# One PSUM bank in four quarters for the small users of the gated stages, and the planner's new price for float32r matmuls

## The chip, the cores and the metric

The kernel runs on 1 core of one Trainium2 chip. The metric is device microseconds of the program; the profile is one execution, taken by the hardware profiler, with times counted from the start of its span. PE is TensorE (PEld its weight loads), DVE is VectorE, ACT is ScalarE, POOL is GpSimd, SP is SyncE, which issues most DMAs. PSUM, where PE writes its results, has eight banks of 512 float32 words in each of 128 partitions; DVE and ACT read and write it too.

## The reference

The input is 4 sequences of 1024 rows of 128 values. Six stages change it in place, each by a residual add. Cut to what matters:

```python
x = x + 0.5 * ffn0(layernorm(x))     # 128 -> 512 -> 128, gelu
x = x + attn0(layernorm(x))          # 16 heads of 8
x = x + 0.5 * ffn0(layernorm(x))
x = x + 0.5 * ffn1(layernorm(x))     # gated stage, below
x = x + attn1(layernorm(x))          # 16 heads of 64, causal
x = x + 0.5 * ffn1(layernorm(x))     # gated stage

def ffn1(x):                         # two layers, l = 0 and 1
    for l in range(2):
        h = shift_token(x)           # upper 64 values from the row before
        q, k, v = split(h @ wqkv[l])             # 8 heads of 64
        q, k = rotary(l2norm(q) * qs[l], l2norm(k) * ks[l])
        x = x + local_attention(q, k, v) @ wo[l]  # windows of 64, own and previous
        h = layernorm(shift_token(x)) * lg[l] + lb[l]
        a, g = split(h @ w1[l] + b1[l])           # 341 each
        x = x + (a * gelu(g)) @ w2[l] + b2[l]
    return x
```

## The kernel before, in words

**Tiles.** `X[i]` holds 512 rows as four parts of 128, for i from 0 to 7. A gated stage (`ffn1`, run as `ffn1a` and `ffn1b`) works on `Y(i)`, one part at a time in the attention: `attend(t0, l, g, ...)` is one frame, 32 parts in each of two layers, 64 frames in a stage. The gated feed-forward, `gated(t0, l, i)`, takes a whole block of four parts; it is done in groups of blocks, between runs of frames, and there are 16 of them in a stage.

**One frame.** `turn_x` transposes the frame's shifted part into PSUM; `upper` (ACT) and `lower` (DVE) copy it out as two float32r parts of one number. `project` makes three times three matmuls of 128x512. `square` (ACT), `turn_a` and `turn_b` (DVE) read a projection; `add` and `normalise` (POOL) finish q and k. `sums` (DVE) writes the 16 squared norms of a frame into PSUM, where `variance` (DVE) has put one or two variances of layer norms; `clip` (DVE), `log`, `guess` (ACT) and `newton` (three DVE instructions) make reciprocal roots of all of them in place. `turn` and `untwist` transpose q and k, `score` makes the scores in two banks of their own, `top`, `exp`, `inverse`, `norm_e` the softmax, `turn_e` and `untwist_e` transpose it, `weigh` multiplies by v. `project_out` makes the 128x128 output product, `collect` (DVE) adds it. A frame also turns, by `turn_x`, one part for the gated feed-forward. There, `bias2` (POOL) adds a bias to `Y(i)` and has to wait until the block's `shift` (five or more DMAs on SP) has read it; `hidden`, `gelu`, `gate`, `down` and `collect` follow. `shift_of` is a small product that `glu_weights` makes four times in a stage.

**Who decides the order.** Every function is recorded with `at(t, f)` as a step. Then `Plan.order` lists them anew: a step becomes ready when the steps that it needs are done and its buffers have a place; engines take the earliest ready step, ties by due time. `best_order` does this six times, each with due times from the try before, and keeps the order with the earliest end by the planner's own clock. `cost` prices an instruction for that clock. So any price and any place moves steps in all stages. The order is then the program's: each engine runs its instructions in it (`follow`), and stands at a wait.

**Where PSUM results go.** All of PSUM is one tile, `wordsP`. `bank(tag, slots)` gives a buffer a place among the banks named, here banks 0 to 5 for everything in a gated stage but the scores (6 and 7). A place is a list of `Cell`s, one to each bank. A buffer keeps its place until its last reader is done. `order` also keeps, for each cell, when each engine last used it, so that a step on another engine starts after that:

```python
for b in banks:
    for c in b.slot:
        for x, end in c.last.items():
            if x != e:
                t = max(t, end + self.X_LAT)
```

All recorded instructions are issued at one line of `issue` (L241), so the groups below are told apart by engine, tile and shape.

Of the kernel before, what the change touches and what calls it, by code (L numbers as in the profile page):

```python
# [11 lines left out]
F32 = mybir.dt.float32  # L12
# [9 lines left out]
D = 128  # L22
EPS = 1e-5
NEG = -1e30
MARGINS = (0.0,)

BANKS, ROUNDED, SWING, WORDS = 4096, 14208, 10240, 28744
# [17 lines left out]
def flat(x):  # L45
    return x.rearrange("p a b -> p (a b)")


def free_size(x):
    return math.prod(x.shape[1:])  # L50
# [42 lines left out]
class Plan:  # L93
# [13 lines left out]
    def __init__(self, ctx, tc):  # L107
        nc = tc.nc
        self.tc, self.ctx, self.pools, self.swing = tc, ctx, {}, ExitStack()
        self.steps, self.recording, self.cur, self.states = [], True, None, []  # L110
        self.scratch, self.owner = bacc.Bacc("TRN2", target_bir_lowering=False, num_devices=1), {}
        self.tags = {}
        self.bank_cells = [Cell("P", 512 * k, 512 * k + 512) for k in range(8)]
        self.masks, self.last, self.table = {}, {}, None
        self.pe, self.ac, self.ve = Engine(self, nc.tensor, "P"), Engine(self, nc.scalar, "A"), Engine(self, nc.vector, "D")
        self.gp, self.sy = Engine(self, nc.gpsimd, "G"), Engine(self, nc.sync, "S")
# [38 lines left out]
    def place(self):  # L155
# [8 lines left out]
        for g in sorted(tags, key=lambda g: (g.last - g.first < 0.9 * total, -g.words, g.first)):  # L164
# [3 lines left out]
            for _ in range(min(g.bufs, len(g.buffers))):  # L168

                for margin, kind in ((m, kind) for m in MARGINS for kind in kinds):  # L170
                    lo = 0
# [20 lines left out]
    def bank(self, tag, slots, shape=(128, 512), dt=F32, turns=True):  # L192
        if self.recording:
            g = self.tags.setdefault(tag, Tag(tag))
            n = (math.prod(shape[1:]) * (2 if dt == BF else 4) + 2047) // 2048
            g.turns = turns
            if not g.slots:
                g.words, g.bufs, g.kind = 0, 0, "P"
                g.slots = [self.bank_cells[k : k + n] for k in slots]
            return self.record("P", g, shape, dt)  # L200
        return self.shaped(shape, dt)

    def await_place(self, x):

# [111 lines left out]
    def cost(self, key, name, args, kw, out, ins, mode):  # L316

        n = free_size(out)
        if key == "P":
            if name == "transpose":  # L320
                return 0.109 if args[1].dtype == F32 else 0.056
            x = args[2]
            if x.dtype == F32:
                t = 4 * free_size(x) / 2400 + 0.009
            elif x.dtype == FR:
                t = max(free_size(x) / 2400 + 0.015, 0.112)
            else:
                t = free_size(x) / 2400 + 0.003

            return t * mode[0] * mode[1] / 128**2  # L330
        if key == "A":
            extra = sum(isinstance(kw.get(z), bass.AP) for z in ("bias", "scale", "accum_out"))
            return 0.055 + n / 1200 + 0.093 * extra
        if key == "D":
            if name in ("tensor_reduce", "bn_stats"):
                n = free_size(ins[0])
            psum = any(self.owner[x.tensor.name].space == "P" for x in (out, *ins) if x.tensor.name in self.owner)
            if name == "tensor_copy" and (not psum or out.dtype == ins[0].dtype == BF):
                n /= 2
            return 0.068 + n / 960 + 0.06 * sum(isinstance(x, bass.AP) and free_size(x) == 1 < n for x in args[1:])  # L340
        if key == "G":
            if name == "tensor_tensor":
                return 0.15 + n * (1.67 if any(x.ap[-1][0] == 0 for x in ins) else 2.1) / 1000
            return 0.245 + n * 0.83 / 1000
        return math.prod(out.shape) * 4 / 360e3
# [302 lines left out]
class Macaron:  # L648
# [491 lines left out]
    def attn1(self, ph, T0, lead):  # L1140
# [197 lines left out]
        def heads(t0, n, i):  # L1338
# [16 lines left out]
            def top(z, k):  # L1355
# [3 lines left out]
                if parts[z].stop < TK:  # L1359
# [4 lines left out]
                    out=sc(), in0=sc(), in1=W["cm"][:, 512 - w : 512], scale=-1.0,  # L1364
                    scalar=V["m", K, k][0][:, 0:1] if two else -NEG,
                    op0=ALU.add, op1=ALU.min, accum_out=o,
# [141 lines left out]
    def ffn1(self, ph, T0, last):  # L1508

        pre = ph + "."  # L1510
        V, at, pe, ac, ve, gp, sy, tile_ = self.begin(pre)
        a, plan = self.a, self.plan
        NB, G, HC = self.NBLK, self.NBLK * 4, 114
        bank = lambda: plan.bank(pre + "p", [0, 1, 2, 3, 4, 5], (128, 4, 128))
        dm = sy.dma_start
        W = {}

# [58 lines left out]
        def glu_weights(t0, l):  # L1576
            def new():
                W["lg", l], W["lb", l] = tile_([128, 1], "lg"), tile_([128, 1], "lb")
                dm(out=W["lg", l], in_=a["L1_ffn_ln_g"][l].unsqueeze(1))
                dm(out=W["lb", l], in_=a["L1_ffn_ln_b"][l].unsqueeze(1))  # L1580

                W["w1h", l], W["w1l", l] = tile_([128, 2, 3 * HC], "w1h", 1, FR), tile_([128, 2, 3 * HC], "w1l", 1, FR)
                W["b2", l] = tile_([128, 128], "b2")
                dm(out=W["b2", l], in_=a["L1_ffn_b2"][l].unsqueeze(0).broadcast_to([128, 128]))

            def clear():
                W["b1", l], W["w2", l] = tile_([128, 6], "b1"), tile_([128, 3, 128], "w2")
                gp.memset(W["b1", l], 0.0)
                gp.memset(W["w2", l][96:128, 2, :], 0.0)

            def second():
                for c in range(3):
                    m = min(HC, 341 - HC * c)
                    dm(out=W["w2", l][0:m, c, :], in_=a["L1_ffn_w2"][l][HC * c : HC * c + m, :])

            def clear_first(z):
                W["w1", l, z] = tile_([128, 512], "raw", 3)
                gp.memset(W["w1", l, z][:, 341:342], 0.0)

            def fetch(z):  # L1600
                dm(out=W["w1", l, z][:, 0:341], in_=a["L1_ffn_w1"][l][:, 341 * z : 341 * z + 341])
                for c in range(3):
                    m = min(HC, 341 - HC * c)
                    o = 341 * z + HC * c
                    dm(out=W["b1", l][0:m, 3 * z + c : 3 * z + c + 1], in_=a["L1_ffn_b1"][l][o : o + m].unsqueeze(1))

            def high(z):
                ac.activation(W["w1h", l][:, z, :], W["w1", l, z][:, 0 : 3 * HC], AF.Copy, scale=W["lg", l])

            def low(z):  # L1610
                w, h = W["w1", l, z][:, 0 : 3 * HC], W["w1h", l][:, z, :].bitcast(F32)
                ve.scalar_tensor_tensor(W["w1l", l][:, z, :], w, W["lg", l], h, ALU.mult, ALU.subtract)

            def shift_of(z):
                pb = W["pb", l, z] = flat(bank())
                for c in range(3):
                    pe.matmul(pb[0:HC, c : c + 1], W["w1", l, z][:, HC * c : HC * c + HC], W["lb", l], start=True, stop=True)

            def bias(z):
                b1, zs = W["b1", l], slice(3 * z, 3 * z + 3)  # L1620
                ve.tensor_tensor(b1[0:HC, zs], W["pb", l, z][0:HC, 0:3], b1[0:HC, zs], ALU.add)

            for j, f in enumerate((new, clear, second)):
                at(t0 + j, f)
            for z in range(2):
                for j, f in enumerate((clear_first, fetch, high, low, shift_of, bias)):
                    at(t0 + 3 + 4 * z + j, f, z)
# [56 lines left out]
                at(t + 0.01, shift_first, key, i)  # L1684

        def turn_x(key, src):
            V["t", key] = bank()
            pe.transpose(V["t", key][:, 0, :], src(), self.ident)

        def upper(key, dst):  # L1690
# [43 lines left out]
        def attend(t0, l, g, xn, xx, xg):  # L1734

            at = lambda t, *z: plan.at(warp(t), *z)
            i, t = divmod(g, 4)
            n = g % 8
            K = (l, g)
# [16 lines left out]
            width = 16 + len(extra)  # L1756

            def sums_of():
                if ("ss", K) not in V:

                    V["ss", K] = [flat(b)[:, 32 * j : 32 * j + width] for b in (bank(),) for j in range(2)]
                return V["ss", K][0]

            def sums():
# [146 lines left out]
                ac.copy(V["oT", K], V["o", K])  # L1911

            def project_out():
                pw = V["w", K] = bank()
                for c in range(4):
                    pe.matmul(pw[:, 0, :], V["oT", K][:, c, :], W["wo", l][:, c, :], start=(c == 0), stop=(c == 3))

# [38 lines left out]
            for k, x in enumerate(extra):  # L1956
                z = x[0]
# [93 lines left out]
        for f in range(2 * G):  # L2051
            l, g = tile_of(f)
# [5 lines left out]
            if g % 4 == 3:  # L2058
# [3 lines left out]
                q = next(q for q in groups if l * NB + i in q)  # L2062
                k = groups.index(q)
# [37 lines left out]
def _constants():  # L2101
# [5 lines left out]
    c = {"c_ident": np.eye(128, dtype=f), "c_blk8": (i[:, None] // 8 == i[None, :] // 8).astype(f)}  # L2107
    c["c_causal"] = np.where(i[None, :] > i[:, None], f(NEG), f(0))
    p, kk = (i % 64)[:, None], i[None, :]
# [55 lines left out]
```

## Time and profile before

| what | value |
| --- | --- |
| median of 3 runs | 3156.43 us (3156.14 to 3158.03) |
| the profiled execution | 3154.36 us, span 3152.6 us |
| granted TensorE clock, mean | 0.987 |
| PE, ACT, DVE, POOL busy | 94%, 78%, 70%, 46% of the span |
| `ffn0a`, `attn0`, `ffn0b` | to about 605 us |
| `ffn1a` | about 605 to 1345 us |
| `attn1` | about 1345 to 2400 us |
| `ffn1b` | about 2400 us to the end |

The stages overlap at their borders. A line of the page's groups reads: line, engine, operation, tiles out<-in, shapes, count, then busy time, mean ns of one, and the idle time of the engine just before them with what ended it. A line of a timeline reads: start, length, engine, operation, count, and in brackets the idle time before it with its releaser.

### The profile page before, as it was taken

The page shows a single profiled execution, that of the slowest core. Times are in us where ns is not written, and L with a number is a line of the kernel's source. Part 1 is how long each engine was busy: PE and PEld are TensorE (multiplying, and loading weights), DVE is VectorE, ACT ScalarE, POOL GpSimd, SP SyncE. Part 2 cuts the span into 40 slices and gives each one's busy share as a digit, 9 for nine tenths or more (in the row PEclk, how much of TensorE's full clock was granted, in tenths as well). Part 3 has the DMA queues.
Part 4 walks back from the last instruction along what each step waited for, and adds up shares of the span by engine and source line. Part 5 has one row for each costly group of instructions (what it writes and reads, how often), then busy time and mean ns, then how long its engine had stood idle before and what let it go on. Part 6 is the DMA issues. An engine that isn't in the chain of part 4 may idle for free.

```text
span 3152.6 us, 75646 instructions
## 1 busy us (share of the span) xinstructions
PE 2973.4 (94%) x26596; PEld 2112.5 (67%) x26596; DVE 2201.5 (70%) x6896; ACT 2461.8 (78%) x6856; POOL 1455.6 (46%) x1622
## 2 busy tenths in 40 slices
PE   8999999988899999899999999999999898999988
PEld 6322222677777777777777777777777677777767
DVE  8343341567767676888888877878787777776775
ACT  6999999678878687767777777777777788787873
POOL 1000000178958586533333333333344898685871
PEclk9999999999999999999999999999999999999999
DMA  1000000122212121122222221222231322122211
GB/s 41 1 1 1 1 3 11 33 67 58 55 40 60 42 59 35 48 59 51 56 46 46 53 46 44 54 46 50 48 81 38 75 57 56 38 59 49 57 42 34
DMA packets 209425, 137.26 MB, mean 44 GB/s; under 512 B 148548, under 2 KB 164632, under 8 KB 209048
## 3 DMA queue, kind: packets, MB, share of 16 engines
q1 hardware_dynamic: 208328, 131.87, 18.4%
q8 instruction: 213, 3.49, 0.4%
q0 software_dynamic: 720, 0.56, 0.1%
q14 instruction: 164, 1.34, 0.1%
HBM read 17.58 MB, written 2.10 MB: 6 GB/s over the span
## 4 chain that ended last, share of the span: by engine, by line
PE 66%; DVE 15%; ACT 8%; POOL 5%; issue 4%; SPq 1%; DMA 1%; DVEq 0%; ACTq 0%; POOLq 0%
PE wordsP L241 66%; DVE wordsS L241 9%; ACT wordsS L241 6%; POOL wordsS L241 4%; DVE words L241 3%; DVE wordsP L241 2%; ACT words L241 2%; POOL words L241 1%; SPq L241 1%; DVE wordsR L241 1%; DMA wordsS<-wordsS 0%; DMA words<-L_ffn_w 0%; ACT wordsR L241 0%; DMA wordsS<-L_attn_x 0%; DVEq L241 0%
## 5 line engine op out<-in xcount | busy, mean ns | idle before, releaser
L241 PE MATMUL wordsP<-wordsS 128*128 128x128 f32 (+7 forms) x11576 | 1567.6, 335 | 109.5 <-POOL wordsS L241 66.5
L241 PEld LDWEIGHTS wordsP<-wordsS 128*128 128x128 f32 (+3 forms) x10296 | 934.3, 145 | 380.0 <-POOL wordsS L241 107.6
L241 ACT ACTIVATE wordsS<-wordsP,wordsS 128x128 f32<-128x128 f32 (+4 forms) x1952 | 926.0, 496 | 317.6 <-PE wordsP L241 212.0
L241 POOL TENSOR_SCALAR wordsS<-wordsS 128x128 f32<-128x128 f32 (+7 forms) x630 | 476.5, 759 | 660.9 <-DVE wordsS L241 491.6
L241 PE MATMUL wordsP<-wordsR 128*128 128x512 f32 (+2 forms) x2592 | 723.7, 410 | 13.9 <-DVE wordsR L241 4.3
L241 POOL TENSOR_TENSOR wordsS<-wordsS 128x512 f32<-128x512 f32 (+1 forms) x512 | 535.4, 1056 | 377.1 <-DVE wordsS L241 330.3
L241 ACT COPY wordsS<-wordsP 128x512 f32<-128x512 f32 (+4 forms) x1040 | 541.9, 540 | 154.3 <-PE wordsP L241 149.7
L241 PE MATMUL wordsP<-wordsS,words 128*64 128x64 f32 (+3 forms) x6216 | 524.4, 299 | 27.6 <-POOL words L241 12.3
L241 PEld LDWEIGHTS wordsP<-wordsR 128*128 128x128 f32 (+1 forms) x2592 | 448.1, 190 | 128.5 <-DVE wordsS L241 13.2
L241 ACT ACTIVATE wordsS<-wordsP 128x1024 f32<-128x1024 f32 (+3 forms) x646 | 506.2, 989 | 16.5 <-PE wordsP L241 14.5
L241 PE MATMUL wordsP<-words 128*128 128x512 f32 (+3 forms) x1540 | 410.9, 373 | 18.8 <-DMA words<-W_vT 9.7
L241 ACT ACTIVATION_READ_ACCUMULATOR wordsS<-wordsP,wordsS 128x1 f32 x1792 | 398.6, 222 | 0.0
L241 DVE TENSOR_TENSOR wordsS<-wordsP,wordsS 128x256 f32<-128x256 f32 (+3 forms) x560 | 256.1, 464 | 169.0 <-PE wordsP L241 134.4
L241 PEld LDWEIGHTS wordsP<-wordsS,words 128*64 128x64 f32 (+2 forms) x5704 | 302.8, 136 | 105.7 <-issue 51.7
L241 DVE TENSOR_REDUCE wordsS<-wordsP 128x4 f32<-128x512 f32 (+1 forms) x512 | 348.3, 682 | 33.1 <-PE wordsP L241 31.8
L241 DVE COPY wordsS<-wordsP 128x512 f32<-128x512 f32 (+4 forms) x444 | 238.2, 550 | 181.9 <-PE wordsP L241 179.0
L241 DVE TENSOR_TENSOR words<-wordsP,wordsS 128x256 f32<-128x256 f32 (+1 forms) x448 | 228.1, 530 | 108.6 <-PE wordsP L241 74.9
L241 DVE CUSTOM_DVE_ANT_0 wordsP<-wordsP,wordsS 128x128 f32<-128x128 f32 (+3 forms) x512 | 264.1, 527 | 30.2 <-PE wordsP L241 20.6
L241 PEld LDWEIGHTS wordsP<-words 128*128 128x128 f32 x1540 | 239.9, 190 | 55.9 <-ACT wordsS L241 23.1
L241 PEld LDWEIGHTS <-wordsS 64*128 64x128 bf16 (+1 forms) x1280 | 63.3, 94 | 279.3 <-issue 263.2
L241 PEld LDWEIGHTS wordsP<-words,wordsS 64*64 64x64 f32 (+1 forms) x4672 | 184.1, 141 | 66.7 <-issue 50.4
L241 PE MATMUL wordsP<-words,wordsS 64*64 64x128 f32 (+1 forms) x4672 | 223.2, 277 | 4.3 <-ACT wordsS L241 1.9
(64 smaller groups left out, 2409.4 us busy)
## 6 DMA issues: line engine op xcount, KB each, us to landing
words<-words SPq DMA_DIRECT2D x648, 128.0 KB
wordsS<-words SPq DMA_DIRECT2D x88, 128.0 KB
wordsS<-wordsS SPq DMA_DIRECT2D x48, 128.0 KB
wordsS<-wordsS SPq DMA_DIRECT2D x48, 112.0 KB
wordsS<-c_rot SPq DMA_DIRECT2D x16, 256.0 KB
wordsS<-L_attn_x SPq DMA_DIRECT2D x8, 256.0 KB
words<-wordsS SPq DMA_DIRECT2D x16, 128.0 KB
out_dram<-wordsS SPq DMA_DIRECT2D x8, 256.0 KB
```

What stands on the lines that cost most here:

```text
L241: self.follow(engine, getattr(engine.engine, name)(*args, **kw))
```

## The change

A new constant names bank 5 as the divided one. Its cell is replaced by four cells of 128 words, and `quarter` gives a buffer one of these. In the gated stages, four kinds of buffers take a quarter: the turned parts (`turn_x`), the norm sums (`sums_of`), the output product (`project_out`), and the shift sums (`shift_of`); the rest of the stage has banks 0 to 4. Stages that used bank 5 whole take all four cells. The planner's price for a float32r matmul changes from n/2400 + 0.015 us, at least 0.112, to n/2400 + 0.021, at least 0.114. Kinds and counts of the instructions that compute stay; their order and places are planned anew.

```diff
+QUARTERED = 5
...
-        self.bank_cells = [Cell("P", 512 * k, 512 * k + 512) for k in range(8)]
+
+        quarters = [Cell("P", 512 * QUARTERED + 128 * k, 512 * QUARTERED + 128 * k + 128) for k in range(4)]
+        self.bank_cells = [quarters if k == QUARTERED else [Cell("P", 512 * k, 512 * k + 512)] for k in range(8)]
...
-                g.slots = [self.bank_cells[k : k + n] for k in slots]
+                g.slots = [[c for cells in self.bank_cells[k : k + n] for c in cells] for k in slots]
             return self.record("P", g, shape, dt)
         return self.shaped(shape, dt)
+
+    def quarter(self, tag, shape=(128, 1, 128)):
+
+        if self.recording:
+            g = self.tags.setdefault(tag, Tag(tag))
+            if not g.slots:
+                g.words, g.bufs, g.kind = 0, 0, "P"
+                g.slots = [[c] for c in self.bank_cells[QUARTERED]]
+            return self.record("P", g, shape, F32)
+        return self.shaped(shape, F32)
...
             elif x.dtype == FR:
-                t = max(free_size(x) / 2400 + 0.015, 0.112)
+                t = max(free_size(x) / 2400 + 0.021, 0.114)
...
-        bank = lambda: plan.bank(pre + "p", [0, 1, 2, 3, 4, 5], (128, 4, 128))
+        bank = lambda: plan.bank(pre + "p", [0, 1, 2, 3, 4], (128, 4, 128))
+        quarter = lambda: plan.quarter(pre + "q")
...
-                pb = W["pb", l, z] = flat(bank())
+                pb = W["pb", l, z] = flat(quarter())
...
         def turn_x(key, src):
-            V["t", key] = bank()
+            V["t", key] = quarter()
...
-                    V["ss", K] = [flat(b)[:, 32 * j : 32 * j + width] for b in (bank(),) for j in range(2)]
+                    V["ss", K] = [flat(b)[:, 32 * j : 32 * j + width] for b in (quarter(),) for j in range(2)]
...
             def project_out():
-                pw = V["w", K] = bank()
+                pw = V["w", K] = quarter()
```

## The prediction

> **What bounds the kernel now.** I read the page first: its busy shares and its slices.
>
> ```profile
> span 3152.6 us, 75646 instructions
> ...
> PE 2973.4 (94%) x26596; PEld 2112.5 (67%) x26596; DVE 2201.5 (70%) x6896; ACT 2461.8 (78%) x6856; POOL 1455.6 (46%) x1622
> ...
> PE   8999999988899999899999999999999898999988
> ...
> PE 66%; DVE 15%; ACT 8%; POOL 5%; issue 4%; SPq 1%; DMA 1%; DVEq 0%; ACTq 0%; POOLq 0%
> ```
>
> PE sets the time: 94% busy and two thirds of the chain that ended last. In the slices all 8s but the first stand at 9 to 17 and 32 to 40: the two gated stages, the only ones whose code the change edits. The table by stretches, for a window inside each:
>
> ```profile
> 620.00:1310.00 690.00, 633.05 (x6996) 511.57 (x6996) 508.08 (x1512) 534.02 (x1898) 506.95 (x513) 0.97 0.24 53
> 2400.00:3100.00 700.00, 635.94 (x7134) 512.06 (x7133) 510.49 (x1516) 546.72 (x1959) 517.90 (x527) 0.97 0.23 51
> ```
>
> After each length come PE, PEld, DVE, ACT, POOL: PE idles 57 and 64 us; DVE and ACT have a quarter free. Over both stages to their ends (1441 us) PE idles 127 us. Who ends it, in the view of waits (PE, first window):
>
> ```profile
> PE wordsP L241 <- POOL wordsS L241: 27.7, 22, 5.8
> PE wordsP L241 <- ACT wordsS L241: 11.8, 16, 2.2
> PE wordsP L241 <- POOL words L241: 7.4, 5, 3.5
> ```
>
> Mostly POOL, in few long waits. The timeline shows what one is:
>
> ```profile
> 747.16 1.26 POOL L241 TENSOR_TENSOR wordsS<-wordsS,words 128x512 f32<-128x512 f32 x1 [2.51 <-DMA wordsS<-wordsS]
> 748.38 1.04 POOL L241 TENSOR_TENSOR wordsS<-wordsS 128x512 f32<-128x512 f32 x1
> 749.38 1.26 POOL L241 TENSOR_TENSOR wordsS<-wordsS,words 128x512 f32<-128x512 f32 x1
> ...
> 751.69 1.54 PE L241 MATMUL wordsP<-wordsS 128*128 128x128 f32 x6 [4.54 <-POOL wordsS L241]
> ```
>
> POOL stood 2.51 us in front of `bias2` (the adds with `words`) until a block's shift DMAs had landed; the normalising products queued behind it came late, and PE lost 4.54 us. No bank is in that chain.
>
> **What the change takes away: bank pressure.** Setting the recorded steps against the trace gives how long each buffer holds its bank. The users that move to quarters (norm sums, turned parts, output products, the shift sums) hold 1638 bank-us in 1441 us, 1.14 banks on average; the others hold 3611, 2.5 banks. So 3.6 of 6 banks are held before; afterwards 2.5 of 5 whole ones. All six are held 10% of the time, and PE idles 26 us of its 127 in those moments. Gain: between 0 and 26 us. I take a third, 9 us: 79 us of the idle time falls while at most four of six are held, so mostly something else is late.
>
> **What it adds: four tenants of one bank.** The planner's clock now keeps engines apart by quarter, but the built program still keeps them apart by bank. Following the semaphores of the changed program, I found 4939 pairs in which an engine touches one quarter after another engine touched another one, and in all of them a wait orders the two. Each is a wait that the plan does not know of. The profile has whole-bank ordering already, between plain readers:
>
> ```profile
> L241 ACT ACTIVATE words<-wordsP 128x512 f32<-128x512 f32 x128 | 76.4, 618 | 16.2 <-PE wordsP L241 7.6 <-DVE wordsS L241 5.2 <-DVE words L241 2.3
> ```
>
> These squares read a projection's bank that DVE also reads and take nothing from DVE, yet waited 5.2 us for it. What will hold the shared bank, and how long:
>
> ```profile
> L241 DVE TENSOR_REDUCE wordsP<-words 128x16 f32<-128x1024 f32 x64 | 78.1, 1220 | 0.8
> ...
> L241 ACT CAST wordsR<-wordsP 128x128 fp32r<-128x128 f32 x121 | 35.0, 291 | 11.6 <-PE wordsP L241 11.2
> ```
>
> (`sums` and `upper`; `lower` has 281 ns in the same table, and a `newton` triple takes some 0.56 us.) The timeline shows an instance:
>
> ```profile
> 836.57 1.22 DVE L241 TENSOR_REDUCE wordsP<-words 128x16 f32<-128x1024 f32 x1
> ...
> 836.75 1.76 PE L241 MATMUL wordsP<-wordsS 128*128 128x128 f32 x16
> ```
>
> Before, the sums and the output product that opens PE's run of 16 lie in two banks and overlap. In one bank PE stands until 837.79 + 0.05 (the usual time from a DVE or ACT end to a PE start): 1.1 us, with all later PE work behind it.
>
> Going through the trace and treating those users as one bank, each access waiting for the latest of another engine and buffer: 92 of 256 turns wait 37.9 us, 33 of 128 output products 24.7 us, 3 of 8 shift sums 1.9 us. PE total 64.5 us. Waits for `sums`, `newton` and `lower` lead. This holds for the order before; the changed order is another. Counting in both orders how much PE work stands between an access and the one before it, priced with the same durations, gives 118.5 us before and 94.2 after: less crowded by 0.79. So 64.5 × 0.79 = 51 us. Ends: 94 us (leads as the order has them), and 20 us, if three fifths fall into waits that PE has anyway. I keep all 51, because PE is the busiest engine and 8.8% idle can hide little.
>
> On the other engines the same count makes DVE wait 124 us and ACT 62 us (`variance` behind output products 47 times, `upper` behind `newton` 38 times). Behind such a wait stand turnings and maxima on DVE, exponentials and copies on ACT, and PE waits for these. PE's waits for DVE and ACT are 20 us in the first window (11.8 for ACT wordsS, 3.6 for DVE wordsS and four smaller ones) and 25 in the second stage; 186 us are 9% of those engines' 2099 us of work. Waits grow faster than the load, so twice that: 18% of 45, 8 us; from 0 to 45.
>
> The Trainium skill speaks against the division: "PSUM — Partial Sum Buffer", section "PSUM bank collisions raise a hardware error", says that PSUM has to be guarded by bank and 32-partition quadrant, not by address, as disjoint columns collide too. By it the quarters are one resource, the +59 of this part; if addresses decided, this part would be 0 and the time 3135. No row before shows two engines in one bank at once.
>
> **What moves.** The order is planned anew everywhere. `bias2`: over 13 block pairs, PE work between the shift DMAs' issue and `bias2` foretells the PE wait, about 8 us less that lead (3.4 gave 3.5 to 4.9, 6.0 gave 1.7, 7.6 gave 1.4). The waits sum to 45.5 us. In the changed order the leads mostly rise (3.8 to 6.2, 3.4 to 4.7, 4.3 to 6.0, one 7.6 to 21.5; three fall, by 0.4 to 1.2), and the rule gives 28 where it gave 42 before: 14 less, from 0 to 14; I take 12, as quarter waits eat some lead. Waits are the only cost here: instruction counts on every engine are equal, DMAs too.
>
> The two cost numbers add no work. Back-to-back 128x512 float32r matmuls start 232 ns apart (median); the old price is 228, the new 234. They reorder the other stages, where PE idles only 11 us from 100 to 600 and 16 us from 1400 to 2300. I take 0, from −8 to +8.
>
> **Sum.** The profiled execution took 3154.4 us (span 3152.6), 2.1 below the median. 3154.4 + 51 + 8 − 9 − 12 = 3192.4; with 2.1 for the median, 3194.5, said 3194.
>
> **Rivals.**
> - Faster. Freed banks let the planner run PE ahead over its waits, and the quarter waits fall into idle time: 20 − 26 − 14 = −20, 3136. It decides where the quarter waits cost PE under 40 us in all. For it: all six banks are held 10% of the time, and PE work is what is short. Against it: the longest waits are POOL's behind a DMA, with banks free. Chance 0.25, with the case that the shared bank hardly orders anything.
> - Even: 21 to 40 us of quarter waits against as much gain, 3150 to 3163. 0.08.
> - Far slower: the leads in the changed order hold as written and DVE's waits pass on whole, 94 + 45 − 21 = +118, 3275. For it: DVE would be 73% busy plus 9%. Against it: an engine held up arrives later at its next conflict, so these waits don't all add. 0.07.
>
> **How the numbers follow.** The forecast, slower through quarter waits (3163 to 3250), has 0.60. Range: 3132 (just below the faster rival) to 3250; outside lie the far slower case and the faster rival's own tail, some 0.15. Under 0.2% (6 us) this kernel's runs can't tell a change from none. Faster 0.25, same 0.08, slower 0.67.
>
> **What would show it.** Right: PE waits in the gated stages for the engines that touch the shared bank (DVE wordsP, which stood at 0.9 us here, and ACT wordsR) rise to tens of us, short and many; `upper`, `lower` and the 128x1 writes show idle time in front; PE busy in these stages drops below 90% of the window; attn1 stays within 8 us. The `bias2` waits shrink by 10 us or so. Wrong: waits on wordsP stay small and PE idles less than 127 us in these stages, or the time moves in the stages that keep their banks.

## The result, and the profile after

The changed kernel took 3212.7 us (median of 4 runs, 3210.0 to 3216.1), the kernel before 3157.2 beside it: ratio 1.0173, 95% interval 1.0156 to 1.0191, slower by 55 us. The profiled execution took 3216.1 us, span 3214.3.

The page:

```profile
span 3214.3 us, 75468 instructions
...
PE 2984.6 (93%) x26520; PEld 2120.5 (66%) x26596; DVE 2226.3 (69%) x6896; ACT 2470.9 (77%) x6856; POOL 1454.9 (45%) x1622
...
PE   8999999988898989899999999999999988989889
...
PE 49%; DVE 15%; ACT 6%; issue 3%; POOL 2%; SPq 0%; DMA 0%; DVEq 0%; ACTq 0%; POOLq 0%
```

PE has the same work (11 us more busy time), but the span is 62 us longer, and the 8s of the slices grow from eight to eleven in the gated stages and nowhere else. The same windows as before, PE's busy time again the first number after the length:

```profile
620.00:1310.00 690.00, 609.35 (x6533) 490.42 (x6566) 485.71 (x1417) 505.01 (x1766) 476.30 (x483) 0.96 0.22 48
2400.00:3100.00 700.00, 621.92 (x6750) 496.56 (x6787) 514.03 (x1498) 538.08 (x1886) 499.45 (x514) 0.98 0.23 50
```

PE idles 81 and 78 us where it idled 57 and 64. Who ends PE's waits, over the whole run (us in total, times, longest), before:

```profile
PE wordsP L241 <- POOL wordsS L241: 66.5, 56, 5.8
PE wordsP L241 <- DVE wordsS L241: 13.3, 24, 2.3
PE wordsP L241 <- DVE wordsR L241: 5.3, 6, 2.6
PE wordsP L241 <- DVE wordsP L241: 1.4, 2, 0.9
```

and after:

```profile
PE wordsP L254 <- POOL wordsS L254: 38.5, 43, 4.4
PE wordsP L254 <- DVE wordsS L254: 36.3, 54, 2.3
PE wordsP L254 <- DVE wordsP L254: 26.0, 28, 2.2
PE wordsP L254 <- DVE wordsR L254: 19.7, 22, 2.6
...
PE wordsP L254 <- ACT wordsR L254: 6.6, 11, 1.3
```

POOL's few long waits shrank, and DVE now ends many short ones. wordsP written by DVE is the norm sums, wordsR is `lower` (DVE) or `upper` (ACT). The groups by shape, in the first gated stage, show the tenants of the divided bank waiting too:

```profile
L254 DVE TENSOR_REDUCE wordsP<-words 128x16 f32<-128x1024 f32 x64 | 78.3, 1224 | 3.4 <-PE wordsP L254 1.3 <-ACT wordsR L254 0.2 <-ACT words L254 0.2
...
L254 ACT CAST wordsR<-wordsP 128x128 fp32r<-128x128 f32 x136 | 35.7, 281 | 29.3 <-PE wordsP L254 20.3 <-DVE wordsP L254 3.3 <-DVE wordsS L254 2.9
...
L254 DVE TENSOR_SCALAR wordsP<-wordsS 128x1 f32<-128x1 f32 x72 | 11.4, 158 | 35.1 <-PE wordsP L254 27.3 <-ACT wordsR L254 5.2 <-ACT wordsS L254 1.9
```

The 128x1 writes of the variances take nothing from PE, yet they stood 27.3 us behind it. Before, the same 72 had almost no idle time in front:

```profile
L241 DVE TENSOR_SCALAR wordsP<-wordsS 128x1 f32<-128x1 f32 x72 | 11.0, 153 | 0.5 <-ACT wordsS L241 0.5
```

One place on the timeline:

```profile
1178.97 1.23 DVE L254 TENSOR_REDUCE wordsP<-words 128x16 f32<-128x1024 f32 x1
...
1180.35 0.30 PE L254 MATMUL wordsP<-wordsS 128*128 128x128 f32 x1 [1.18 <-DVE wordsP L254]
...
1180.68 0.29 DVE L254 TENSOR_TENSOR wordsR<-wordsP,wordsR 128x128 fp32r<-128x128 f32 x1 [0.48 <-PE wordsP L254]
```

`sums` writes its quarter until 1180.20; the turn, with another quarter and nothing to take from the sums, starts 0.15 us later, and PE has stood 1.18 us. Then `lower` on DVE, which reads the part of another turn in a third quarter, waits 0.48 us for this turn: one wait makes the next.

Matching PE's recorded steps to the trace, PE's idle time in both gated stages is, by the step that it stands in front of (worked out from the trace and the planner's order; no view gives it):

| idle before (us) | before | after |
| --- | --- | --- |
| turns (`turn_x`) | 8.6 | 78.5 |
| output products, shift sums | 6.2 | 10.2 |
| `turn_e`, `turn` (behind POOL) | 79.8 | 40.1 |
| all | 127.6 | 171.8 |

### The profile page after: what moved, and what is told of

It is laid out like the page before. It is cut to its first block, busy times and chain, and to the rows that moved or that the text cites. A ratio compares the mean times of both kernels' runs of the same rounds, so it can differ in the third digit from the quotient of the medians.

```text
span 3214.3 us, 75468 instructions
## 1 busy us (share of the span) xinstructions
PE 2984.6 (93%) x26520; PEld 2120.5 (66%) x26596; DVE 2226.3 (69%) x6896; ACT 2470.9 (77%) x6856; POOL 1454.9 (45%) x1622
## 4 chain that ended last, share of the span: by engine, by line
PE 49%; DVE 15%; ACT 6%; issue 3%; POOL 2%; SPq 0%; DMA 0%; DVEq 0%; ACTq 0%; POOLq 0%
PE wordsP L254 49%; DVE wordsS L254 7%; DVE wordsP L254 5%; ACT wordsS L254 4%; DVE words L254 2%; POOL wordsS L254 2%; ACT words L254 1%; DVE wordsR L254 1%; POOL words L254 1%; SPq L254 0%; ACT wordsR L254 0%; DMA wordsS<-wordsS 0%; DMA words<-words 0%; ACT wordsP L254 0%; DMA words<-L_ffn_b 0%
## 5 line engine op out<-in xcount | busy, mean ns | idle before, releaser
L254 PE MATMUL wordsP<-wordsS 128*128 128x128 f32 (+6 forms) x11515 | 1552.7, 334 | 134.6 <-POOL wordsS L254 38.5
L254 PEld LDWEIGHTS wordsP<-wordsR 128*128 128x128 f32 (+1 forms) x2592 | 458.9, 192 | 126.8 <-issue 9.0
L254 PE MATMUL wordsP<-words 128*128 128x512 f32 (+3 forms) x1540 | 412.9, 374 | 19.5 <-DMA words<-W_vT 10.3
```

Of the source, the lines that this page charges most:

```text
L254: self.follow(engine, getattr(engine.engine, name)(*args, **kw))
```

## The experiments

Two theories: A, PE and the norm sums stand in each other's way in the shared bank; B, the order as planned anew (fewer whole banks, another price) is worse in itself. Every time is a median; ratios are to the kernel before on the same chip, with 95% intervals.

**Price alone.**

```diff
-                t = max(free_size(x) / 2400 + 0.015, 0.112)
+                t = max(free_size(x) / 2400 + 0.021, 0.114)
```

> The kernel before with the new price of float32r matmuls alone; no quarters, six whole banks. Theory A (the shared bank's waits cost the time): no quarter, no cost, 3157 us within 8 us (3149 to 3165). Theory B (the order as planned anew is worse in itself, price included): up to the whole +56 us, 3165 to 3213. PE's waits for DVE wordsP stay near 1 us in a gated stage under A.

3133.9 us, ratio 0.9923 (0.9907 to 0.9939): faster, which neither theory had. PE idles 108.7 us in the gated stages; `turn_e`, which waits for POOL, 27.1 us instead of 53.4. The largest of PE's waits, those for POOL, fell from 66.5 us over the whole run:

```profile
PE wordsP L241 <- POOL wordsS L241: 39.0, 47, 3.8
```

So the half of B that is the price falls, with its sign reversed, and the division has to be measured against 0.992 too: it costs 0.0250 of 3157, 79 us. The other half, the order for fewer whole banks, is left for the third run.

**The order of before, with a shared bank.**

```diff
         steps = self.best_order()
+        self.replace(steps)
```

(`replace`, not shown, keeps the order and gives the buffers other places: the small ones quarters of bank 5, the rest banks 0 to 4.)

> Order of the kernel before, step for step, old price; only the places of PSUM buffers are dealt out again after the order is fixed: turned parts, norm sums, output products and shift sums go to quarters of bank 5, the rest to banks 0 to 4 (3 of 1768 buffers find no such place and lie in the other kind). Theory A: this order has not been planned for quarters at all and is the more crowded of the two, 64.5 us of direct PE waits by the trace before plus some 8 through DVE and ACT: 3157 + 73 = 3230 us, 3200 to 3270. Theory B: the order is that of before, so 3157 within 10 us.

3283.6 us, ratio 1.0395 (1.0378 to 1.0413). Not one step changed its position, and 125 us were added. The view of PE's waits, whole run:

```profile
PE wordsP L241 <- POOL wordsS L241: 60.4, 54, 6.0
PE wordsP L241 <- DVE wordsS L241: 57.2, 59, 2.9
PE wordsP L241 <- DVE wordsP L241: 45.8, 47, 3.7
```

POOL's share is nearly the 66.5 us of before; DVE's two were 13.3 and 1.4. Before turns, products and shift sums PE idles 117.6 us (14.8 before). The large buffers were moved into five banks as well, but PE's idle time as a whole rose by 89 us (267.9 against 179.2), less than the 103 us before these steps alone; so the added idle time is the shared bank's. The rest of the longer span is 40 us of PE's own busy time (3013.8 against 2973.4).

**The order of the changed kernel, spread.** A `replace` of the opposite kind: small buffers get whole banks where five suffice.

> Order of the changed kernel, step for step; only places are dealt out again: 252 of the 520 small buffers get a whole one of banks 0 to 4 where one is free through their life, 268 stay in quarters of bank 5, and 180 of those overlap another there. Theory A: some two thirds of the quarter waits go, so about 56 x 0.65 = 36 us come back: 3177 us, 3160 to 3190; if the order itself also carries a gain (fewer long waits behind the bias additions), below 3165. Theory B: the order costs, so 3213 within 10 us.

3143.8 us, ratio 0.9945 (0.9929 to 0.9962). With the same order, dealing places out again gives 72 us back (1.0173 to 0.9945), double what was expected, though 180 buffers still overlap in bank 5. So the order by itself is not slower than that of before, and B falls. Idle time before turns falls to 19.6 us.

**The planner told of the bank.**

```diff
             c.free, c.time, c.last, c.held = True, 0.0, {}, None
+        last = {}
+        for c in self.bank_cells[QUARTERED]:
+            c.last = last
```

> The changed kernel, but the planner's clock keeps one record of last uses for all four quarters, so it plans with the waits that the program will have. Theory A: the waits are still there, but the order is chosen around them: part of the +56 comes back, 3165 to 3200 us, PE waits for DVE wordsP and wordsR below 20 us over both gated stages (43 in the changed kernel). If only the lack of knowledge costs and a quarter is as good as a bank: 3157 or below, down to 3137 with the freed banks. Theory B (fewer whole banks and the price make the order worse): 3213 within 15 us.

3186.0 us, ratio 1.0082 (1.0059 to 1.0105): about half of the 55 us back. The plan itself shows what this knowledge is worth: run alone, the planner ends its order at 3121 us by its own clock before the change, at 3060 with the quarters, and at 3122 with this edit. Its gain of 61 us was a belief that quarters are independent. But the waits did not fall as expected:

```profile
PE wordsP L254 <- DVE wordsP L254: 38.0, 39, 5.4
PE wordsP L254 <- ACT wordsS L254: 37.5, 59, 2.4
```

DVE wordsP rose from 26.0 to 38.0 us over the whole run. Here, planning with the waits did not avoid them. Whether the plan accepts them or real times drift from planned ones was not tried.

**The division alone.** Both kernels' difference without the price line.

> The changed kernel with the old price: the division alone. The price alone gave 0.992 of before, the two together 1.017, so if they simply add, the division costs 79 us and this runs at 3157 + 79 = 3236 us (3215 to 3260). If instead the price only removes waits that the quarters remove anyhow (bank pressure behind the bias additions), the division alone costs about what the two cost together: 3213 within 10 us. Theory B (division free, order by chance): 3157 within 10 us.

3219.3 us, ratio 1.0189 (1.0172 to 1.0206): the two edits do not add. (The planner went through five passes here; with the new price the changed kernel goes through all six.) Before `turn_e` PE idles 22.8 us with the old price and 22.2 with the new one: the order planned for quarters already lacks the POOL waits that the price removes with whole banks.

**Norm sums alone in quarters.**

```diff
-            V["t", key] = quarter()
+            V["t", key] = bank()
...
-                pw = V["w", K] = quarter()
+                pw = V["w", K] = bank()
```

(and the shift sums.)

> New price; only the norm sums take quarters of bank 5, turned parts, output products and shift sums go to banks 0 to 4. PE then writes nothing into the shared bank during a gated stage. If the cost is PE standing behind DVE and ACT in a shared bank, nearly all of the 79 us against the price alone goes: 3125 to 3150 us, and it may beat the price alone (3134) as bank pressure falls. If the cost is having five whole banks, or DVE and ACT holding each other up in bank 5: 3170 or more.

3129.8 us, ratio 0.9910 (0.9895 to 0.9925). The cost is gone and five whole banks suffice. Idle before turns and products: 10.3 us.

**Norm sums out, the others in quarters.**

```diff
-                    V["ss", K] = [flat(b)[:, 32 * j : 32 * j + width] for b in (quarter(),) for j in range(2)]
+                    V["ss", K] = [flat(b)[:, 32 * j : 32 * j + width] for b in (bank(),) for j in range(2)]
```

> New price; the norm sums take whole banks 0 to 4, turned parts, output products and shift sums stay in quarters of bank 5. In the changed kernel PE's waits before a turn were ended by instructions on the norm sums (sums, clip, newton) for 35 of 78 us, by lower and upper of another turn for 16. If the tenants share the cost as these waits do, about half of 79 us stays: 3134 + 40 = 3174 us, 3155 to 3190. If the sums with their 1.22 us are nearly all of it: below 3150. If turns and products alone collide as much: over 3195.

3317.3 us, ratio 1.0502 (1.0487 to 1.0518), over every expectation, and misleading. The planner's second pass ran into a dead end (no step could get its place), so the program has the first, unrefined order. The number says nothing of the tenants, and it makes the passes a suspect in every comparison: the old price with six banks hits a dead end in the fifth pass and keeps the fourth's order; the new price goes through all six.

**Is it the price or the passes?** A price half way, and the new price held to four passes (`TRIES = 4`).

> The kernel before with a price half way, n/2400 + 0.018 us and at least 0.113. Matmuls of 128x512 start every 232 ns by the trace: the old price says 228, this one 231, the new one 234. If the gain of the price alone (-25 us) comes from pricing them near the truth, this gains as much: 3125 to 3142 us. If a price only shuffles the order and the gain is chance, the time may lie anywhere from 3125 to 3175, with 3142 to 3175 the likelier part.

3134.3 us, ratio 0.9925 (0.9910 to 0.9940), all six passes; as much as with 0.021.

> The kernel with the new price alone, its planner held to four passes of best_order. With the old price the fifth pass runs into a dead end, so the order of the kernel before is the best of four; with the new price all six go through and the sixth is kept. If the gain of the price (-25 us) is those two passes, this runs at 3157 us, 3145 to 3170. If the price itself gains, 3134 within 8 us.

3144.4 us, ratio 0.9964 (0.9951 to 0.9976). Four passes give 11 of the 24 us; the last two give the other 13. The first 11 remain with the price or with chance.

**Norm sums out, with an order that was refined.**

> Norm sums in whole banks 0 to 4, turned parts, output products and shift sums in quarters of bank 5, as in the run with the sums out, but with the price 0.018, with which six passes of the planner go through (with 0.021 the second pass ran into a dead end, and the order was the unrefined first one). Six whole banks with this price took 3134. If the 3317 us of that run were the tenants of the shared bank, this takes about as long, over 3250. If they were the unrefined order, the shared bank costs what its tenants' waits come to: with turns and products alone 3134 + 40 = 3174 us, 3150 to 3195.

(The price is 0.018 here.) 3122.3 us, ratio 0.9891 (0.9876 to 0.9906): the fastest of all, 1.1% ahead of the kernel before. My 40 us for turns and products in one bank was wrong: they cost nothing that shows in the time. PE's waits, whole run:

```profile
PE wordsP L254 <- ACT wordsS L254: 33.2, 63, 2.4
PE wordsP L254 <- POOL wordsS L254: 26.9, 43, 2.4
PE wordsP L254 <- DVE wordsR L254: 20.1, 25, 2.6
...
PE wordsP L254 <- DVE wordsP L254: 1.1, 3, 0.6
```

Waits for `lower` (wordsR) are as in the changed kernel (19.7); those for the norm sums (wordsP) are gone, and so is most of DVE wordsS (15.7 against 36.3). Idle before turns: 19.5 us instead of 78.5, though more than the 8.6 before. So neither the sums alone nor the turns and products alone cost; only the mixture does.

**Norm sums alone, at 0.018.**

> Norm sums alone in quarters of bank 5, price 0.018; here the fifth pass ends in a dead end and the fourth is kept. PE still writes nothing into the shared bank. Theory A: within 15 us of the same division at 0.021 (3130), 3120 to 3150. If the passes matter as much as the place, 3145 to 3160.

3142.0 us, ratio 0.9951 (0.9937 to 0.9966): 12 us more than at 0.021, with the fourth pass kept. Differences of a dozen us between orders are therefore not to be read as causes. The runs by tenants each have an order of their own too; what separates the mixture from them, 70 to 89 us over the three runs that part them, is several times that.

**Two divided banks.** Sums in bank 5, PE's small users in bank 4.

> Price 0.018 (six passes go through, the fifth is kept). Two divided banks: norm sums alone in quarters of bank 5, turned parts, output products and shift sums in quarters of bank 4; everything else in four whole banks 0 to 3. If the cost of the change is PE's users and the norm sums lying in one bank, this has none of it and frees bank pressure further: 3110 to 3130 us. If turned parts and products cost by themselves and the run with the sums out had luck with its order: 3140 to 3180. If four whole banks are too few for the rest (the trace has 2.5 held on average, five or more 17% of the time in the last run's five): above 3150.

3127.9 us, ratio 0.9898 (0.9881 to 0.9914): no better than the sums in whole banks, no worse. Four whole banks suffice. (The last run's five were all held 13% of the time, not 17%.)

## Why the prediction was right, and where its terms were off

Forecast +38 us, measured +55, inside the range, by the mechanism named. That the sum came so near is partly luck: the quarter waits were put 23 us too low, the gains some 19 too low, and 11 us of longer busy time on PE were not in it ("Waits are the only cost here").

- **Quarter waits on PE, 51 us.** Idle time before the three kinds of PE steps rose from 14.8 to 88.7 us, 74 us. The two factors can be checked apart. The base, 64.5 us for the order of before, was measured by the run with that order: 117.6 − 14.8 = 103 us. The ratio of the two orders, 0.79, came out as 74/103 = 0.72. So the order count was sound, and the base was mis-sized by 1.6. The likely reason, not shown by a run: going through an undisturbed trace counts each conflict alone, and leaves out the waits that a wait makes, as at 1180.68. I had argued against the far slower rival that a held-up engine arrives later, so that waits don't all add; on PE they came to more than the count.
- **Through DVE and ACT, 8 us.** PE idle before `weigh` and inside steps rose from 22.9 to 34.3 us, 11 us. But the trace of the changed kernel has 76 fewer matmul records, and some 5.6 us of this stands inside `score` where they are missing, so about 6 us is left.
- **Gains, 21 us.** Before `turn_e` and `turn` PE idles 40 us less; its waits for POOL fell by 31 us (wordsS 66.5 to 38.5, words 13.1 to 10.1), and how much of that is `bias2` was not separated. Whether freed banks had a part is open: the price alone shortens the idle time before `turn_e` from 53.4 to 27.1 us with six whole banks, the division alone to 22.8.
- **"The two cost numbers add no work ... I take 0".** This step failed. A price acts through the order, and through how many passes the planner survives; alone it gave −24 us, and PE's idle time fell in the gated stages (127.6 to 108.7 us), where the prediction looked only at the division. The other stages did stay: from the last PSUM use of `ffn1a` to the first of `ffn1b` 1068 us before, 1072 after.
- **The signs to look for.** PE under 90% of its window (88% and 89%), DVE wordsP from 1.4 to 26.0 us, the 128x1 writes from 0.5 to 35.1 us idle: right. ACT wordsR (`upper`) was named to rise to tens of us and reached 6.6; it was DVE wordsR (`lower`) that went from 5.3 to 19.7.
- **Which tenants.** The prediction priced all four as one kind. Turns and products with their own readers shared a bank at no cost in time (0.9891), and the sums did (0.9910); put with them, the 1.22 us `sums` and the chain behind them, independent of the turns, make the sharing cost.
- **The rule of the Trainium skill** that was weighed ("PSUM — Partial Sum Buffer", section "PSUM bank collisions raise a hardware error": PSUM guarded by bank, not by address) is how the built program behaves. With the same order, sharing cost 125 us and unsharing gave 72. What the chip does with two engines in one bank at once, no run here shows.

## What to carry to other kernels

A piece of a bank is a place, not a resource: before dividing one, list which engines touch which tenant, and put together only tenants that already follow each other; keep out any that another engine works on independently and for long. When a scheduler plans around a model, vary its prices and count how many passes it completed before crediting a code change, and test a placement with the order held fixed. Conflicts counted on an undisturbed trace can come out low: here they were 0.63 of the real ones.

## What the runs showed of the hardware

PE's own work does not always take the same time. PE's busy time for the same matmuls was 2963.5 us in the run of 3122 us, 2973.4 before, 2984.6 after and 3013.8 with the shared bank in the order of before; the mean granted clock was 0.992, 0.987, 0.983 and 0.975, and PE's idle time 153.6, 179.2, 229.7 and 267.9 us. In these four the clock falls as the idle time grows. It is not a rule of the idle time alone: with the price alone PE idled 161.5 us at 0.985, and in the run with the unrefined order 283.6 us at 0.981. The kernel before alone spread from 0.983 to 0.988 over its executions. The Trainium skill ("TensorE: Matmul & The Clock Gate", Part 1) describes a clock that is gated unless recent activity releases it. The four rows would fit that, but no run here isolates it.
